# The first ffn's transposed input: turned again on TensorE, or read back from DRAM

## The chip, the cores and the metric

The kernel runs on one core of one Trainium2 chip. The core has five engines with a queue each: TensorE (PE, whose weight loads the profile lists as PEld), VectorE (DVE), ScalarE (ACT), GpSimd (POOL) and SyncE (SP, which here only issues DMAs). The metric is the device time of one execution in microseconds (us); less is better.

## What is computed

Two gated blocks follow each other, on x of 4 x 1024 rows with 512 elements. Each block is

```
xn = layernorm(x)
s  = attention(xn)          # layer 0: chunked linear attention, 16 heads; layer 1: softmax attention
g  = silu(ffn(xn))          # layer 0: below; layer 1: gated ffn with integer weights
x  = x + s * g
```

What the change touches is the input of layer 0's ffn:

```
def bitlinear(x, w):                       # used twice in the ffn: w_fc, then w_proj
    xn = (x - mean(x)) / sqrt(var(x) + 1e-6)
    return xn @ ternarize(w).T
h = gelu(bitlinear(xn, w_fc));  y = bitlinear(h, w_proj)
```

So the ffn normalises rows that layer 0's norm has already normalised. With the row's variance v, that is xn times one more factor per row, 1/sqrt(v/(v + 1e-5) + 1e-6).

## The kernel before, in words

The 4096 rows are worked on in NBLK = 8 blocks of BLK = 512 rows, a block in TPB = 4 tiles of 128 rows. The 512 elements of a row are KD = 4 pieces of 128, the contraction pieces of the matmuls.

**Layer 0's attention** (up to 622 us in the profile) goes through 32 steps, four head groups for each block. For each block, `moments0` (L292) takes mean and variance of the four tiles, `norms0` (L302) makes from them a factor that goes straight from x to the ffn's input (`st[:, :, 3]`), and `turn0` (L310) normalises a tile on DVE, turns it on TensorE and copies it with ACT into `xnT`, the transposed block that all projections of the attention read. Each step also makes on POOL the decayed queries `qd` (L357), which `outs` uses one step later, and for odd blocks a copy of the state (L395). The last step (L512 to L514) also prepares the first ffn block: `first_rows` (L453) scales each of four row tiles of x (loaded at L542) on DVE, turns it with four transposes (L463) and has `split_in` (L227) write it as a pair: `hi`, the value rounded to fp32r by ACT, and `lo`, the remainder, by DVE. Both are matmul operands. After it come the last `output` matmuls (L333).

**Layer 0's ffn** (622 to some 1150 us) is a software pipeline over g, 16 slots c = 0 to 15 for each block. In a slot, `hidden` (L587) does eight fc matmuls (L594, the pair hi and lo times four pieces), then on ACT gelu to h (L599), the rounding hp (L604) and the square (L606), on DVE the remainder hp (L607) and the sum of squares (L616), on POOL the sum of h (L615). `proj` (L642) does eight pj matmuls (L647) with the hp of two to eight slots before. PSUM gives fc two banks, h has three buffers. In slots 1, 3, 5, 7 `gate` (L652) finishes a row tile of the previous block: loads of x and s by SP (L659, L661), DVE L664, tanh on ACT L666, DVE L667 and L668, the add of x on POOL L669, the store of x1 by SP (L670), and DVE's bn_stats on it (L105). `stats` (L620) comes in slot 1. `turn_out` (L673), in slots 14 and 15 and the next block's 0 and 2, transposes the result for layer 1 (L684).

The next block's input is made in the same slots: in slots 0, 3, 6, 9 SP loads a row tile of x (`x0f`, L711); in slots 2, 5, 8, 11 `prep_in` (L566) scales it on DVE (`xq`, L574); in slots 3, 6, 9, 12 `turn_in` (L579) has TensorE transpose it (four 128 x 128 matmuls with the identity, L582) and `split_in` writes hi (ACT, L230) and lo (DVE, L231).

In block 0 the last six tiles of the projection's weights are made ternary on DVE beside it (L208, L210).

**What sets the order.** TensorE's order is the program's, written out by hand (`manual_schedule`). On the other engines a planner orders the instructions of each queue by its own estimate of when they are ready; an instruction wrapped in `keep_in_program_order` is put behind the one traced before it on its engine, but later ones may still be put ahead of it. Each engine then runs its queue strictly in order and waits at semaphores. SP's and POOL's DMAs stand in those queues too.

Of the kernel before, what the change touches and what calls it, by code (L numbers as in the profile page):

```python
# [24 lines left out]
NTILE = NT // P  # L25
BLK = 512
TPB = BLK // P
NBLK = NT // BLK
# [7 lines left out]
def kernel(ctx, tc, ins, out):  # L36
    nc = tc.nc
# [17 lines left out]
    def tr(name):  # L55
        return psum.tile([P, 4, P], F32, tag="tr", name=name)
# [6 lines left out]
    ident = const.tile([P, P], F32, tag="ident", name="ident")  # L63
# [15 lines left out]
    def xpair(name):  # L79
        return [xpool.tile([P, KD, BLK], F32, tag=f"xp{n}", name=f"{name}_{n}") for n in range(2)]  # L80
# [61 lines left out]
    def transpose_to(dst, src, name, on_scalar):  # L142

        t = tr(f"tr_{name}")
        for k in range(4):
            nc.tensor.transpose(t[:, k, :], src[:, k * P : (k + 1) * P], ident)
        if on_scalar:
            nc.scalar.copy(dst, t)  # L148
        else:
            nc.vector.tensor_copy(dst, t)  # L150
# [73 lines left out]
            w = nxt  # L224
            yield

    def split_in(xp, i, tp):  # L227

        hi, lo = [a[:, :, i * P : (i + 1) * P] for a in xp]
        nc.scalar.copy(hi.bitcast(F32R), tp)  # L230
        nc.vector.tensor_tensor(lo.bitcast(F32R), tp, hi, ALU.subtract)  # L231


    with ExitStack() as es:
# [6 lines left out]
        xt = {}  # L241
# [45 lines left out]


        xnTs, vs, oTs = {}, {}, {}
        xparts = {}  # L290

        def moments0(blk):  # L292
            st = st0[blk]
            for i in range(TPB):
# [7 lines left out]
        def norms0(blk):  # L302

            st = st0[blk]
            nc.vector.tensor_tensor(st[:, :, 3], st[:, :, 1], st[:, :, 1], ALU.mult)
            nc.vector.tensor_tensor(st[:, :, 3], st[:, :, 3], st[:, :, 2], ALU.mult)
            inv_std(st[:, :, 3], eps6)
            nc.vector.tensor_tensor(st[:, :, 3], st[:, :, 3], st[:, :, 1], ALU.mult)

        def turn0(blk, i):  # L310
            st = st0[blk]
            t = blk * TPB + i
            xn = p2.tile([P, D], F32, tag="xn", name=f"xn0_{t}")
            nc.vector.tensor_scalar(
                xn, xt.pop(t), st[:, i, 0:1], st[:, i, 1:2], ALU.subtract, ALU.mult
            )
            transpose_to(xnTs[blk][:, :, i * P : (i + 1) * P], xn, f"x0_{t}", True)

        def values(blk, i):
            if i == 0:  # L320
# [129 lines left out]
            oTs[blk, g] = p2.tile([P, BLK], F32, tag="oT", name=f"oT0_{nm}", bufs=6)  # L450
            nc.scalar.copy(oTs[blk, g], o)

        def first_rows(i0):  # L453

            st = st0[0]
            for i in range(i0, i0 + 2):
                xq = p2.tile([P, D], F32, tag="xn", name=f"xq_{i}")
                nc.vector.tensor_scalar(
                    xq, xt.pop(i), st[:, i, 0:1], st[:, i, 3:4], ALU.subtract, ALU.mult
                )  # L460
                tp = tr(f"tr_xq_{i}")
                for k in range(KD):
                    nc.tensor.transpose(tp[:, k, :], xq[:, k * P : (k + 1) * P], ident)  # L463
                split_in(xparts[0], i, tp)

        es.enter_context(tc.manual_schedule(engines={mybir.EngineType.PE}))

        st = st0[0]
# [37 lines left out]
        for n, (blk, g) in enumerate(steps):  # L506

            if g < 2:
                jobs = [(output, blk - 1, 2 * g + c) for c in range(2)] if blk else []
            else:  # L510
                jobs = [(values, blk + 1, 2 * g - 4 + c) for c in range(2)] if blk + 1 < NBLK else []
            if n + 1 == len(steps):  # L512
                xparts[0] = xpair("xp_0")
                jobs = [(first_rows, 0), (first_rows, 2)]  # L514
            if g == 0 and blk + 1 < NBLK:
                moments0(blk + 1)
            pts = scores(blk, g, *cur[:2])
            for _ in range(2):
                next(beside, None)
            nxt = None  # L520
            if n + 1 < len(steps):
                nxt = project(*steps[n + 1])
            if jobs:
                jobs[0][0](*jobs[0][1:])
            outs(blk, g, cur[2], pts)
            if nxt:
# [25 lines left out]
    with ExitStack() as es:  # L552
# [5 lines left out]
        def tr0(name):  # L558
            return pp.tile([P, KD, P], F32, tag="tr", name=name)

        hparts, sums, mvs, x1s, xnTp, x0fs = {}, {}, {}, {}, {}, {}
        for c in range(wpj0, NH0):
            wpj.append(p2.tile([P, D], F32R, tag=f"wpj{c}", name=f"wpj{c}", bufs=1))
        rows = p2.tile([P, D], F32, tag="rows", name="rows", bufs=1)

        def prep_in(blk, i):  # L566

            st = st0[blk]
            if i == 0:
                xparts[blk] = xpair(f"xp_{blk}")  # L570
            t = blk * TPB + i
            x = x0fs.pop(t)
            xq = p2.tile([P, D], F32, tag="xq", name=f"xq_{t}")
            nc.vector.tensor_scalar(  # L574
                xq, x, st[:, i, 0:1], st[:, i, 3:4], ALU.subtract, ALU.mult
            )
            return lambda: turn_in(blk, i, xq)

        def turn_in(blk, i, xq):  # L579
            tp = tr0(f"tr_xq_{blk}_{i}")  # L580
            for k in range(KD):
                nc.tensor.transpose(tp[:, k, :], xq[:, k * P : (k + 1) * P], ident)  # L582
            split_in(xparts[blk], i, tp)

        before = None

# [65 lines left out]
        def gate(blk, i):  # L652

            t = blk * TPB + i
            mv = mvs[blk]

            last = blk == NBLK - 1 and i >= 2
            x = p2.tile([P, D], F32, tag="x" if last else "xr", name=f"x0r_{t}")
            nc.sync.dma_start(out=x, in_=x_t[t])  # L659
            s = p2.tile([P, D], F32, tag="xq" if last else "s", name=f"s0_{t}")  # L660
# [7 lines left out]
            nc.vector.scalar_tensor_tensor(th, th, sc, s, ALU.mult, ALU.mult)  # L668
            nc.gpsimd.tensor_tensor(th, th, x, ALU.add)  # L669
            nc.sync.dma_start(out=x1_t[t], in_=th)  # L670
            moments(p2, th, st1[:, t, :], f"c{t}")
# [19 lines left out]
                )  # L691

        es.enter_context(tc.manual_schedule(engines={mybir.EngineType.PE}))
        pending = None
        W = {}
        for g in range(NH0 * NBLK + 2 + 2 * TPB):
            blk, c = divmod(g, NH0)
# [7 lines left out]
                        )  # L705
                    )
            if blk < NBLK:
                if c % 3 == 0 and c < 3 * TPB and blk + 1 < NBLK:
                    t = (blk + 1) * TPB + c // 3
                    x0fs[t] = p2.tile([P, D], F32, tag="x", name=f"x0f_{t}")  # L710
                    nc.sync.dma_start(out=x0fs[t], in_=x_t[t])  # L711
                if c >= 2 and c % 3 == 2 and c < 2 + 3 * TPB and blk + 1 < NBLK:
                    pending = prep_in(blk + 1, (c - 2) // 3)
                hidden(blk, c)
                if blk == 0 and wpj0 + c < NH0:
                    ternary("pj", wpj0 + c, raw0("pj", wpj0 + c, "f"))
            for i in range(TPB):
# [13 lines left out]
                gate(blk - 1, c // 2)  # L731
            if blk and c == 12:
                norm1(blk - 1, p2)
            if pending and c % 3 == 0:
                pending()
                pending = None
# [755 lines left out]
```

## Time and profile before

| | |
|---|---|
| time, median of 3 runs | 3141.68 us (3139.5 to 3142.14) |
| the profiled execution's own time | 3143.35 us |
| its span | 3141.6 us |
| TensorE clock granted, mean | 0.993 |
| layer 0's ffn, a whole block from slot 2 to slot 2 | 65.3 to 66.8 us |
| DVE's operations that the change takes out of the ffn | L574: 28, 731 ns in the mean; L231: 32 with the last step of the attention, 671 ns |
| TensorE's transposes of it | L582: 112, L463: 16 |
| HBM read / written | 104.10 MB / 41.94 MB |

The profile is of one execution. Its page gives each engine's busy time; the windows give the same for chosen stretches; the timeline gives single instructions: start and duration in us, engine, line, output and inputs, and in brackets how long the engine stood idle before it and what ended that. "x8" at the end of a row says that eight such instructions are merged in it. A TensorE row's duration contains the run of the pipeline; the time that a matmul takes from the engine is the distance between starts.

### The profile page before, as it was taken

The numbers are of one execution on the slowest core, as the hardware profiler recorded it, in microseconds if no ns is written. First come the engines' busy times: TensorE is split into PE (matmuls) and PEld (weight loads), VectorE is DVE, ScalarE is ACT, GpSimd is POOL, SyncE is SP. The second block draws the span as 40 slices with busy tenths as digits, with TensorE's granted clock in tenths as the row PEclk, the third lists the DMA queues.
The fourth block names the chain that finished last, engine by engine and source line by source line (L and its number), as shares of the span: only waits on it lengthen the run. The fifth ranks groups of instructions, "written<-read, shape, count | busy, mean of one in ns | idle before, by whom it ended". The sixth has DMA issues, their size and how long they took to land.

```text
span 3141.6 us, 60980 instructions
## 1 busy us (share of the span) xinstructions
PE 3083.5 (98%) x26185; PEld 1762.0 (56%) x26185; DVE 1898.5 (60%) x2622; ACT 1195.6 (38%) x1696; POOL 1501.6 (48%) x615
## 2 busy tenths in 40 slices
PE   9999999999999998999999999999999999999998
PEld 5555555577777874443344444334444435888887
DVE  4444555478887866566655555555555684566655
ACT  3111111155556543444444444444444444333332
POOL 0000000034444444888888898888888970000001
PEclk9999999999999999999999999999999999999999
DMA  3111111112222331100001000100000013322211
GB/s 131 54 54 61 54 54 41 58 54 87 84 74 68 108 127 49 35 9 8 8 17 40 13 11 15 41 14 14 10 17 15 12 44 104 115 77 64 68 51 55
DMA packets 97799, 158.46 MB, mean 50 GB/s; under 512 B 13040, under 2 KB 26864, under 8 KB 97392
## 3 DMA queue, kind: packets, MB, share of 16 engines
q1 hardware_dynamic: 96704, 151.33, 15.6%
q8 instruction: 207, 3.39, 0.5%
q0 software_dynamic: 816, 3.15, 0.3%
q14 instruction: 72, 0.59, 0.1%
HBM read 104.10 MB, written 41.94 MB: 46 GB/s over the span
## 4 chain that ended last, share of the span: by engine, by line
PE 84%; DVE 11%; ACT 2%; issue 2%; POOL 1%; SPq 1%; DMA 0%; ACTq 0%; POOLq 0%; DVEq 0%
PE sk L1033 9%; PE sq L1006 8%; PE y L1052 8%; PE qk L350 7%; PE gate L1224 5%; PE up L1224 5%; PE dn L1246 5%; PE v1ps L862 4%; PE v0ps L324 4%; PE wo L333 3%; PE wo L862 3%; PE wk L862 3%; PE wq L862 3%; PE fc L594 3%; PE pj L647 3%; PE sk L1039 2%
## 5 line engine op out<-in xcount | busy, mean ns | idle before, releaser
L1073 POOL TENSOR_TENSOR part<-part,pT 128x2048 f32<-128x2048 f32 x184 | 844.5, 4590 | 25.8 <-ACT pT L1044 16.8
L1010 DVE TENSOR_REDUCE mx<-sq 128x2 f32<-128x1024 f32 x512 | 603.3, 1217 | 384.1 <-PE sq L1006 383.0
L1044 ACT ACTIVATE pT<-sk 128x1024 f32<-128x1024 f32 x512 | 496.2, 1021 | 618.8 <-PE sk L1039 615.4
L1033 PE MATMUL sk<-wqT,wkT 32*128 32x512 f32 x2048 | 332.7, 645 | 5.2 <-DVE mx L1010 5.1
L1006 PE MATMUL sq<-wkT,wqT 32*128 32x512 f32 x2048 | 322.9, 642 | 7.1 <-ACT pT L1044 5.1
L1052 PE MATMUL y<-pT,v 128*32 128x512 f32 x2048 | 276.3, 610 | 0.2 <-ACT pT L1044 0.2
L615 POOL TENSOR_TENSOR sums<-sums,h 128x512 f32<-128x512 f32 x112 | 164.2, 1466 | 227.3 <-ACT h L599 222.1
L647 PE MATMUL pj<-wpj,hp 128*128 128x512 f32 x1024 | 265.1, 397 | 5.7 <-DVE hp L607 4.9
L594 PE MATMUL fc<-xp,wfc 128*128 128x512 f32 x1024 | 260.9, 397 | 2.9 <-ACT h L599 2.0
L1268 POOL TENSOR_TENSOR th<-th,x 128x512 f32<-128x512 f32 x31 | 40.1, 1293 | 457.9 <-DVE th L1267 377.1
L1039 PE MATMUL sk<-mT,onesr 2*128 2x512 f32 x1024 | 239.8, 788 | 2.2 <-DVE mT L1022 2.2
L357 POOL TENSOR_TENSOR qd<-qT,wqkv 128x512 f32<-128x512 f32 x32 | 40.6, 1270 | 397.5 <-ACT qT L355 372.3
L350 PE MATMUL qk<-xnT,wqkv 128*128 128x512 f32 x512 | 229.9, 602 | 0.7 <-ACT xnT L148 0.7
L647 PEld LDWEIGHTS pj<-wpj,hp 128*128 128x128 f32 x1024 | 190.2, 188 | 57.6 <-DVE hp L607 17.3
L594 PEld LDWEIGHTS fc<-xp,wfc 128*128 128x128 f32 x1024 | 187.5, 188 | 44.2 <-ACT h L599 5.1
L1033 PEld LDWEIGHTS sk<-wqT,wkT 32*128 32x128 f32 x2048 | 99.7, 184 | 138.3 <-issue 110.4
L1071 POOL TENSOR_TENSOR part<-pT,pT 128x2048 f32<-128x2048 f32 x31 | 141.1, 4552 | 74.4 <-ACT pT L1044 74.3
L1224 PE MATMUL gate<-xp,wf 128*128 128x512 f32 x704 | 174.2, 390 | 0.0
L1224 PE MATMUL up<-xp,wf 128*128 128x512 f32 x704 | 173.9, 389 | 0.0
L1246 PE MATMUL dn<-wf,hp 128*128 128x512 f32 x704 | 173.6, 389 | 0.0
L607 DVE TENSOR_TENSOR hp<-h,hp 128x512 fp32r<-128x512 f32 x128 | 118.0, 922 | 76.3 <-ACT hp L604 76.2
L350 PEld LDWEIGHTS qk<-xnT,wqkv 128*128 128x128 f32 x512 | 95.5, 191 | 112.4 <-issue 106.3
(219 smaller groups left out, 4527.0 us busy)
## 6 DMA issues: line engine op xcount, KB each, us to landing
s<-s SPq DMA_DIRECT2D x96, 256.0 KB
x<-x SPq DMA_DIRECT2D x36, 256.0 KB
x<-in_x SPq DMA_DIRECT2D x32, 256.0 KB
raw_fc<-in_w_fcT SPq DMA_DIRECT2D x32, 256.0 KB
x0f<-in_x SPq DMA_DIRECT2D x32, 256.0 KB
x0r<-in_x SPq DMA_DIRECT2D x32, 256.0 KB
x<-th SPq DMA_DIRECT2D x32, 256.0 KB
xnT<-xnT_d SPq DMA_DIRECT2D x8, 1024.0 KB
```

What stands on the lines that cost most here:

```text
L350: nc.tensor.matmul(a, lhsT=wqkv[k][:, c0 : c0 + P], rhs=xnTs[blk][:, k, :], start=(k == 0), stop=(k == KD - 1),)
L594: nc.tensor.matmul(a, lhsT=wfc[k][:, c * P : (c + 1) * P], rhs=xp[n][:, k, :].bitcast(F32R), start=(k == 0 and n == 0), stop=(k == KD - 1 ...
L647: nc.tensor.matmul(ds[i], lhsT=hparts[blk, c][n][:, i * P : (i + 1) * P], rhs=wpj[c], start=(c == 0 and n == 0), stop=(c == NH0 - 1 and n ...
L862: nc.tensor.matmul(out[r0 : r0 + HD, :], lhsT=lhsT[:, r0 : r0 + HD], rhs=rhs, start=start, stop=stop,)
L1006: nc.tensor.matmul(sq[:, hh, :], lhsT=qT[r, q0 : q0 + P], rhs=kT[r, n * 512 : (n + 1) * 512], start=True, stop=True,)
L1010: nc.vector.tensor_reduce(mx[:, qt, 2 * pair : 2 * pair + 2, n], sq, AX.X, ALU.max)
L1033: nc.tensor.matmul(sks[h // 2][:, h % 2, :], lhsT=kT[r, kb * P : (kb + 1) * P], rhs=qT[r, qh * 512 : (qh + 1) * 512], start=True, stop=False,)
L1044: nc.scalar.activation(pT[:, 2 * pair : 2 * pair + 2, :], sks[pair], AF.Exp, scale=QKS)
L1052: nc.tensor.matmul(y[r, :], lhsT=v[:, kb, r], rhs=pT[:, h, :], start=(kb == 0), stop=(kb == TB - 1),)
L1073: add.tensor_tensor(parts[u], parts[u], pT, ALU.add)
L1224: nc.tensor.matmul(a, lhsT=ws[n, c][:, k, :], rhs=xp[m][:, k, :], start=(k == 0 and m == 0), stop=(k == KD - 1 and m == 1),)
L1246: nc.tensor.matmul(ds[i], lhsT=hparts[blk, c][n][:, i * P : (i + 1) * P], rhs=w, start=(c == 0 and n == 0), stop=(c == NH1 - 1 and n == 1),)
```

## The change

The transposed rows that the attention makes anyway are kept. When the last tile of a block is turned, POOL's DMA queue stores the whole `xnT` of the block (1 MB) to a new DRAM tensor `xn0T`; another of its DMAs stores the factor of each row (512 values, now without the first norm's factor in it) to `more`. The ffn's input is then made from these, piece by piece (k = 0 to 3, all 512 rows of 128 elements at once) instead of row tile by row tile: SP loads piece k in slot 3k (and, with the first, the factors, broadcast to 128 partitions); POOL multiplies it by the factors in slot 3k + 3, three slots after its load; in slot 3k + 4 ACT writes hi and POOL writes lo. Loads, scales and splits are kept in program order. For the first block the loads come after the attention's last step but one, and the scales and splits at the end of the last step. TensorE's transposes L463 and L582, DVE's scaling L458 and L574, and DVE's split L231 are no longer there.

```
+    xn0T_d = [
+        dram.tile([KD, P, BLK], F32, tag=f"xn0T{i}", name=f"xn0T_d{i}") for i in range(NBLK)
+    ]
+    more_d = dram.tile([NBLK, BLK], F32, tag="more", name="more_d")
...
-    def split_in(xp, i, tp):
...
+    def ffn_in(blk, k, tile):
+
+        if k == 0:
+            xparts[blk] = xpair(f"xp_{blk}")
+            mores[blk] = tile("more", f"more_{blk}")
+            nc.sync.dma_start(out=mores[blk], in_=more_d[blk].partition_broadcast(P))
+        x = tile("x", f"x0f_{blk}_{k}")
+        tc.keep_in_program_order(nc.sync.dma_start(out=x, in_=xn0T_d[blk][k]))
+
+        def scale():
+            tc.keep_in_program_order(nc.gpsimd.tensor_tensor(x, x, mores[blk], ALU.mult))
+
+        def split():
+            hi, lo = [a[:, k, :] for a in xparts[blk]]
+            tc.keep_in_program_order(nc.scalar.copy(hi.bitcast(F32R), x))
+            tc.keep_in_program_order(
+                nc.gpsimd.tensor_tensor(lo.bitcast(F32R), x, hi, ALU.subtract)
+            )
+
+        return scale, split
...
@@ norms0
-            nc.vector.tensor_tensor(st[:, :, 3], st[:, :, 3], st[:, :, 1], ALU.mult)
+            nc.gpsimd.dma_start(out=more_d[blk].rearrange("(i p) -> p i", p=P), in_=st[:, :, 3])
@@ turn0
             transpose_to(xnTs[blk][:, :, i * P : (i + 1) * P], xn, f"x0_{t}", True)
+            if i == TPB - 1:
+                nc.gpsimd.dma_start(out=xn0T_d[blk].rearrange("k p n -> p k n"), in_=xnTs[blk])
...
-        def first_rows(i0):
...
             if n + 2 == len(steps):
 
-                for i in range(TPB):
-                    xt[i] = p2.tile([P, D], F32, tag="x", name=f"x0f_{i}", bufs=4)
-                    tc.keep_in_program_order(nc.sync.dma_start(out=xt[i], in_=x_t[i]))
+                first_in = [
...
+                    for k in range(KD)
+                ]
+            if n + 1 == len(steps):
+                for m in range(2):
+                    for k in range(KD):
+                        first_in[k][m]()
...
-        def prep_in(blk, i):
...
-        def turn_in(blk, i, xq):
...
             if blk < NBLK:
-                if c % 3 == 0 and c < 3 * TPB and blk + 1 < NBLK:
...
-                    nc.sync.dma_start(out=x0fs[t], in_=x_t[t])
-                if c >= 2 and c % 3 == 2 and c < 2 + 3 * TPB and blk + 1 < NBLK:
-                    pending = prep_in(blk + 1, (c - 2) // 3)
                 hidden(blk, c)
+                if blk + 1 < NBLK and c <= 3 * KD + 1:
+                    if c % 3 == 0 and c:
+                        coming[0]()
+                    if c % 3 == 0 and c < 3 * KD:
+                        nxt = ffn_in(
+                            blk + 1, c // 3,
+                            lambda tag, name: p2.tile([P, BLK], F32, tag=tag, name=name),
+                        )
+                    if c % 3 == 1:
+                        if c > 1:
+                            coming[1]()
+                        coming = nxt
...
-            if pending and c % 3 == 0:
-                pending()
-                pending = None
```

More of the change, by code (lines that the diff above doesn't have):

```diff
@@ L225, in weights0 @@
             yield
-    def split_in(xp, i, tp):
-        hi, lo = [a[:, :, i * P : (i + 1) * P] for a in xp]
-        nc.scalar.copy(hi.bitcast(F32R), tp)
-        nc.vector.tensor_tensor(lo.bitcast(F32R), tp, hi, ALU.subtract)
+    def ffn_in(blk, k, tile):
[14 more added lines that the diff above has]
+        return scale, split
+    xparts, mores = {}, {}
     with ExitStack() as es:
@@ L289 @@
         xnTs, vs, oTs = {}, {}, {}
-        xparts = {}
         def moments0(blk):
@@ L451, in outs @@
             nc.scalar.copy(oTs[blk, g], o)
-        def first_rows(i0):
[L455 to L464, printed above, removed]
         es.enter_context(tc.manual_schedule(engines={mybir.EngineType.PE}))
@@ L511 @@
                 jobs = [(values, blk + 1, 2 * g - 4 + c) for c in range(2)] if blk + 1 < NBLK else []
-            if n + 1 == len(steps):
-                xparts[0] = xpair("xp_0")
-                jobs = [(first_rows, 0), (first_rows, 2)]
             if g == 0 and blk + 1 < NBLK:
@@ L538 @@
             if n + 2 == len(steps):
-                for i in range(TPB):
-                    xt[i] = p2.tile([P, D], F32, tag="x", name=f"x0f_{i}", bufs=4)
-                    tc.keep_in_program_order(nc.sync.dma_start(out=xt[i], in_=x_t[i]))
+                first_in = [
+                    ffn_in(
+                        0, k,
+                        lambda tag, name: p2.tile(
+                            [P, BLK], F32, tag={"more": "xn"}.get(tag, tag), name=name,
+                            bufs={"x": 4}.get(tag, 2),
+                        ),
+                    )
[5 more added lines that the diff above has]
+                        first_in[k][m]()
         for i in range(TPB):
@@ L559, in tr0 @@
             return pp.tile([P, KD, P], F32, tag="tr", name=name)
-        hparts, sums, mvs, x1s, xnTp, x0fs = {}, {}, {}, {}, {}, {}
+        hparts, sums, mvs, x1s, xnTp = {}, {}, {}, {}, {}
         for c in range(wpj0, NH0):
@@ L564 @@
         rows = p2.tile([P, D], F32, tag="rows", name="rows", bufs=1)
-        def prep_in(blk, i):
[L568 to L577, printed above, removed]
-        def turn_in(blk, i, xq):
[L580 to L583, printed above, removed]
         before = None
@@ L659, in gate @@
             nc.sync.dma_start(out=x, in_=x_t[t])
-            s = p2.tile([P, D], F32, tag="xq" if last else "s", name=f"s0_{t}")
+            s = p2.tile([P, D], F32, tag="more" if last else "s", name=f"s0_{t}")
             nc.sync.dma_start(out=s, in_=s0_t[t])
@@ L707 @@
             if blk < NBLK:
-                if c % 3 == 0 and c < 3 * TPB and blk + 1 < NBLK:
-                    t = (blk + 1) * TPB + c // 3
-                    x0fs[t] = p2.tile([P, D], F32, tag="x", name=f"x0f_{t}")
-                    nc.sync.dma_start(out=x0fs[t], in_=x_t[t])
-                if c >= 2 and c % 3 == 2 and c < 2 + 3 * TPB and blk + 1 < NBLK:
-                    pending = prep_in(blk + 1, (c - 2) // 3)
-                hidden(blk, c)
+                hidden(blk, c)
+                if blk + 1 < NBLK and c <= 3 * KD + 1:
[5 more added lines that the diff above has]
+                            lambda tag, name: p2.tile([P, BLK], F32, tag=tag, name=name),
+                        )
+                    if c % 3 == 1:
+                        if c > 1:
+                            coming[1]()
+                        coming = nxt
                 if blk == 0 and wpj0 + c < NH0:
@@ L733 @@
                 norm1(blk - 1, p2)
-            if pending and c % 3 == 0:
-                pending()
-                pending = None
             if 0 < blk < NBLK and c >= 14:
```

## The prediction

> **What bounds the kernel.** I read the granted clock first (0.993, so nothing is throttled), then the page's busy times, then, by windows, the stage that the change touches: the first ffn, 622 to 1150 us.
>
> ```profile
> PE 3083.5 (98%) x26185; PEld 1762.0 (56%) x26185; DVE 1898.5 (60%) x2622; ACT 1195.6 (38%) x1696; POOL 1501.6 (48%) x615
> ```
>
> TensorE is busy all the time, so whatever leaves it should shorten the kernel, unless another engine is the one that paces a stretch. I number a block's slots c = 0 to 15 (one group of eight fc and eight pj matmuls each). From the first fc of slot 2 to that of slot 13 (the gate of the previous block lies there) the windows of blocks 1 to 7 are:
>
> ```profile
> core 0: us, PE busy (x) PEld busy (x) DVE busy (x) ACT busy (x) POOL busy (x), PEclk, DMA share, GB/s
> 690.87:734.68 43.81, 43.14 (x195) 34.46 (x194) 40.06 (x64) 23.79 (x40) 23.41 (x15) 1.00 0.31 91
> 756.21:801.24 45.03, 44.03 (x198) 34.70 (x198) 41.15 (x64) 24.34 (x41) 23.12 (x15) 1.00 0.35 111
> 822.78:867.81 45.03, 44.07 (x199) 34.70 (x198) 41.15 (x64) 24.32 (x41) 23.06 (x15) 1.00 0.35 112
> 889.35:934.64 45.29, 44.33 (x198) 34.62 (x198) 41.13 (x64) 24.32 (x41) 23.05 (x15) 1.00 0.37 111
> 956.19:1001.21 45.02, 44.10 (x199) 34.69 (x198) 41.14 (x64) 24.32 (x41) 23.06 (x15) 1.00 0.36 111
> 1022.75:1067.36 44.61, 43.78 (x198) 34.78 (x198) 40.49 (x64) 24.36 (x41) 22.73 (x15) 1.00 0.36 113
> 1088.90:1131.44 42.54, 41.82 (x182) 33.35 (x182) 36.48 (x59) 22.68 (x38) 22.16 (x15) 1.00 0.31 100
> ```
>
> DVE is busy 41 of 45 us: it has no room. The last row prepares no next block, so it is a trial of the removal made inside this profile. An undisturbed slot takes 3.67 us (fc starts 834.80 and 838.47) and one with four transposes 4.13 (879.75 to 883.88), so 0.45 us for a set. TensorE alone would need 11 x 3.67 + 0.45 = 40.8 us in the last row; it took 42.54. Even without input work it waits 1.7 us, and for this:
>
> ```profile
> 1119.91 1.80 DVE L668 SCALAR_TENSOR_TENSOR th<-th,mv,s 128x512 f32<-128x512 f32 x1
> 1121.64 0.68 DVE L607 TENSOR_TENSOR hp<-h,hp 128x512 fp32r<-128x512 f32 x1
> 1122.24 1.77 DVE L616 TENSOR_TENSOR sums<-sums,sq 128x512 f32<-128x512 f32 x1
> ```
> ```profile
> 1119.87 1.30 POOL L615 TENSOR_TENSOR sums<-sums,h 128x512 f32<-128x512 f32 x1 [3.28 <-ACT h L599]
> 1121.79 1.67 POOL L669 TENSOR_TENSOR th<-th,x0r 128x512 f32<-128x512 f32 x1 [0.63 <-DVE th L668]
> ```
> ```profile
> 1122.37 1.89 PE L647 MATMUL pj<-wpj,hp 128*128 128x512 f32 x7 [0.25 <-DVE hp L607]
> ```
>
> These are the timelines of DVE, POOL and PE. A DVE operation with two SBUF inputs that meets a POOL operation takes 1.8 us, the same one free of it 0.68 (L616, L607) or 0.74 (L668); the hp that this holds back is what pj waits for. In these slots the stage is paced by DVE, and POOL lengthens DVE.
>
> **The change part by part.**
>
> Removed on PE: 28 sets of L582 transposes, 0.45 us each, 12.6 us, and 4 sets of L463. The latter's second pair stands bare at the end of the attention (wait from 605.7, next matmul 607.28): 1.6 us. The first pair lies beside DVE's pt (602.09 to 604.57), for which PE waits anyway: nothing.
>
> Removed on DVE: per block four xq (L574, 731 ns mean) and four splits (L231, 671 ns), 5.6 us, three of each in the gate window. What that is worth the last row says: 42.54 against 45.0 us (mean of blocks 2 to 6) is 2.5 us, of which four transposes are 1.8; the DVE operations, partly lying in its waits for ACT's th (3.1 us), give only 0.7. L308 (8 x 565 ns) goes too, in the attention, where DVE waits for PE: 0. ACT's cast stays, from SBUF instead of PSUM (L803 619 ns against L230 575): 4 x 0.05 us per block beside 38 busy of 66: 0.
>
> Added on POOL: per block four scales and four subtractions, 128x512 two-input fp32, as L615 (1.29 us alone). No row shows POOL writing fp32r; on DVE the type costs nothing (L607 as L616), so I take 1.29. POOL has room, busy 28 of a block's 66 us. The price is what they do to DVE. In the last row's window the excess of DVE's operations over their free times is 10 x (1.118-0.68) + 11 x (0.977-0.68) + 4 x (1.538-0.74) = 10.9 us for 15 POOL operations: 0.72 us each. The Trainium skill (SBUF — State Buffer, Who interferes with whom) has it harder: the pair of ports is locked for a whole instruction and the loser blocks fully. By that rule an added operation may cost up to 1.29 us, and six in slots 3 to 10 7.7 us a block; by the row 6 x 0.72 = 4.3. The lower end is 0, where the operation meets DVE reading PSUM (y L664, 734 ns always) or waiting. I take the row: same operations, same slots. Scale and subtraction of slots 12 and 13 meet a DVE that has caught up: 0.
>
> Added waits: the subtraction waits on POOL for ACT's cast, which stands behind h, hp and sq of its slot; queued behind it are the next sums and the gate's add (L669), for which DVE's bn_stats (L105) waits, with hp behind it and pj behind that. In the sum this counts as 0 beyond the 0.72; the third case prices it. The cast waits for a scale that is a slot older: 0.
>
> SP: a block gets five loads (four and the broadcast) for four, at 0.33 us issue. Pinned behind the gate's stores (issued 834.36, 849.92, 859.12 in block 3's gate), a load lands some 2.4 us later (as x0r does in the chain), 7 to 10 us before the sums of the slot whose scale takes it: hidden; cover gone, the scale, the sums behind it and the free h buffers would be late. SP's stores of x1 are not moved.
>
> The stores, on POOL's queue in the attention: 8 of 1 MB and 8 of 2 KB in 4-byte pieces. The three weight loads there issue in 0.75 to 0.91 us and land in 5.7 to 9.4. For the small ones no row is near; between 0 and a few us I take 0.9. They are read some 500 us later. Behind them on POOL stand qd (L357) and the state copy (L395), which idle 372 and 154 us for their inputs in all, and qd is used a step (18 us) later. Taken at 0; the upper end, every issue late for PE, is 16 x 0.9 = 14 us, which qd's idle time excludes nearly wholly.
>
> The sum, in us. Blocks 1 to 6: before 268.8 (the six rows); after, by the last row, 42.1 (block 1 has one transpose set less) + 5 x 42.54 + 6 x 4.3 = 280.6: +11.8. Block 0 has no gate: 4 x 0.45 of transposes and PE's one 1.88 wait for xq go, two POOL operations meet DVE's ternary work (2 x 0.72): -2.3. End of the attention -1.6. In all +7.9. The profiled execution took 3143.35 (span 3141.6 and 1.75 around it) and would take 3151.3; it is 1.7 above the median, so on the median 3149.6, say 3150.
>
> **The rivals.**
>
> *Faster: POOL's operations fall in gaps.* Place: slots 3 to 10. POOL idles 21 us of the last window, much of it while DVE does y, bn_stats or waits for ACT. At 1 us a block instead of 4.3: 254.8 + 6 - 268.8 = -8.0, block 0 -3.7, attention -1.6: 3128; at 0, 3122. It decides below 3.0 us a block, 0.5 per operation, where the sum is zero. For it: six of the last window's ten L616 are free. Against: h, which starts sums, also starts hp, and the pinned operations follow sums directly, when DVE's two-input work runs.
>
> *Slower still: the gate's add behind a waiting subtraction.* If in slots 4 and 7 the queue has the subtraction first, L669 comes 1.3 us later twice a block: 6.9 us a block, 254.8 + 41.4 - 268.8 - 3.9 = +23.5: 3165. For it: bn_stats already waits for L669 once (1.2 us, last row). Against: the subtraction may be queued behind L669.
>
> *It does nothing that shows:* DVE's order is changed and the price comes out near 3.0: 3142.
>
> **How the numbers follow.** Sum as reckoned 0.45 (3143 to 3158), gaps 0.30 (3122 to 3136), late add 0.17, nothing 0.08. About 0.2% is what a measurement of this kernel tells from no change, 3135 to 3148: gaps give faster 0.29; same takes the last case and the lower edge of the first, 0.19; slower 0.52. Range over the signs 3124 to 3166; the likeliest case's own is 3143 to 3158.
>
> **What would show it.** Right: L582, L574, L231 gone; windows from slot 2 to 13 of blocks 1 to 6 near 46.8 us with PE waiting for hp L607; L616, L607 and L668 longer in the mean; last block unchanged at 42.5; fc starting 1.6 us earlier than 622.05. Gaps: windows at 43 to 44. Late add: waits of L105 for L669 over 1 us per block. Wrong altogether: PE waiting for xp or SP's loads, or for qd in the attention, or POOL's fp32r operation well over 1.3 us.

## The result, and the profile after

| | before | after |
|---|---|---|
| median (runs shown beside each other) | 3141.2 us (4 runs, 3139.5 to 3142.1) | 3182.8 us (4 runs, 3171.7 to 3186.4) |
| ratio, 95% interval | | 1.0129 (1.0115 to 1.0143) |
| profiled execution: time, span | 3143.35, 3141.6 us | 3171.73, 3170.0 us |
| first fc | 622.05 us | 624.14 us |
| block 0, from first fc to slot 2 of block 1 | 68.82 us | 69.21 us |
| blocks 1 to 6, from slot 2 to slot 2 | 398.0 us | 429.4 us |
| from slot 2 of block 7 to the end | 2052.7 us | 2047.2 us |

The change made the kernel 1.3% slower, outside the forecast range. The four rows below are differences of starts in the two traces: +2.1, +0.4, +31.4 and -5.5 us, together the 28.4 us between the spans. The last one lies where no operation was changed, only the name of one buffer. The changed kernel, measured once more (last experiment), took 3176.5 us; by the two ratios the loss is some 34 to 41 us.

The page of after, engines' busy time and number of instructions:

```profile
PE 3068.1 (97%) x26057; PEld 1745.7 (55%) x26057; DVE 1927.3 (61%) x2550; ACT 1196.9 (38%) x1696; POOL 1624.1 (51%) x695
```

TensorE lost its 128 transposes and 15 us of busy time. DVE lost 72 operations and is busy 29 us longer: the operations that stayed grew. That alone says where to look.

The windows of after: blocks 1 to 3 and 7 from slot 2 to slot 13, as in the prediction, and slot 14 of block 2 alone.

```profile
core 0: us, PE busy (x) PEld busy (x) DVE busy (x) ACT busy (x) POOL busy (x), PEclk, DMA share, GB/s
697.57:743.00 45.43, 41.49 (x176) 32.38 (x175) 41.56 (x46) 23.85 (x40) 33.85 (x22) 1.00 0.29 93
764.03:810.94 46.91, 42.39 (x182) 33.16 (x182) 41.15 (x57) 24.36 (x41) 31.17 (x20) 1.00 0.34 108
835.79:882.73 46.94, 42.38 (x183) 33.15 (x182) 41.16 (x57) 24.36 (x41) 31.22 (x20) 1.00 0.33 108
1122.75:1165.29 42.54, 41.82 (x182) 33.32 (x182) 36.48 (x59) 22.66 (x38) 22.17 (x15) 1.00 0.31 100
814.61:822.05 7.44, 4.25 (x22) 3.23 (x20) 6.96 (x18) 2.19 (x4) 3.73 (x3) 1.00 0.11 35
```

The gate's window takes 46.9 us, as forecast (46.8), against 45.0 before: DVE is as busy as before (41.15 us) with fewer operations (57 for 64). The last block is the same to the hundredth. But the window is less than half of the loss: a block is 5.2 us longer (71.76 against 66.57) and the window only 1.9. The other 3.3 us are slot 14, 7.44 us against 4.03 in block 2 of before (slot 13 gives 0.1 us back). There TensorE's fc starts are 805.01 and 809.04, and the transposes between them wait for nothing:

```profile
805.01 1.99 PE L594 MATMUL fc<-xp,wfc 128*128 128x512 f32 x8
806.83 2.02 PE L647 MATMUL pj<-wpj,hp 128*128 128x512 f32 x8
808.69 0.60 PE L684 MATMUL tr_x<-ident,xn 128*128 128x128 f32 x4
809.04 2.09 PE L594 MATMUL fc<-xp,wfc 128*128 128x512 f32 x8
```

The chain of slot 14 in after, from the timelines of TensorE, ACT, DVE and POOL in block 2:

```profile
816.43 2.02 PE L645 MATMUL pj<-wpj,hp 128*128 128x512 f32 x8
821.64 0.66 PE L682 MATMUL tr_x<-ident,xn 128*128 128x128 f32 x4 [3.19 <-ACT xn L677]
```
```profile
820.77 1.52 ACT L677 ACTIVATE xn<-th,shift,st 128x512 f32<-128x512 f32 x2 [5.18 <-DVE shift L143]
```
```profile
810.29 1.78 DVE L605 TENSOR_TENSOR hp<-h,hp 128x512 fp32r<-128x512 f32 x1
812.00 1.78 DVE L614 TENSOR_TENSOR sums<-sums,sq 128x512 f32<-128x512 f32 x1
813.70 1.79 DVE L605 TENSOR_TENSOR hp<-h,hp 128x512 fp32r<-128x512 f32 x1
815.41 1.78 DVE L614 TENSOR_TENSOR sums<-sums,sq 128x512 f32<-128x512 f32 x1
817.12 1.25 DVE L125 TENSOR_SCALAR rw_n<-st 128x4 f32<-128x4 f32 x1
...
820.57 0.16 DVE L143 SCALAR_TENSOR_TENSOR shift<-st 128x4 f32<-128x4 f32 x1
```
```profile
809.79 3.45 POOL L613 TENSOR_TENSOR sums<-sums,h 128x512 f32<-128x512 f32 x2
813.19 1.75 POOL L242 TENSOR_TENSOR x0f<-x0f,more 128x512 f32<-128x512 f32 x1
814.91 1.74 POOL L613 TENSOR_TENSOR sums<-sums,h 128x512 f32<-128x512 f32 x1
816.60 1.73 POOL L248 TENSOR_TENSOR xp<-x0f,xp 128x512 fp32r<-128x512 f32 x1
```

Read upwards from TensorE: the transposes of the finished tile wait 3.19 us for ACT's xn, this for DVE's `shift`, the last operation of norm1 (L125 to L143, here from 817.12), and norm1 stands behind hp and sums of slots 11 and 12, each at 1.78 us instead of 0.68. Even its first operation, of 128 x 4 elements, takes 1.25 us instead of 0.16: it ends when POOL's does. POOL beside them runs without a gap, each operation at 1.74 instead of 1.29. The starts on both engines are 1.7 us apart: the two take turns. So a POOL operation here costs DVE 1.7 - 0.6 = 1.1 us, and POOL is late as well: the last scale and subtraction, planned for slots 12 and 13, run in slots 13 and 14 (which begin at 810.94 and 814.61).

### The profile page after: what moved, and what is told of

The parts are those of the page before. It is cut to its first block, busy times and chain, and to the rows that moved or that the text cites. A ratio compares the mean times of both kernels' runs of the same rounds, so it can differ in the third digit from the quotient of the medians.

```text
span 3170.0 us, 60776 instructions
## 1 busy us (share of the span) xinstructions
PE 3068.1 (97%) x26057; PEld 1745.7 (55%) x26057; DVE 1927.3 (61%) x2550; ACT 1196.9 (38%) x1696; POOL 1624.1 (51%) x695
## 4 chain that ended last, share of the span: by engine, by line
PE 80%; DVE 10%; issue 4%; ACT 2%; POOL 2%; DMA 1%; SPq 1%; ACTq 0%; POOLq 0%; DVEq 0%
PE sk L1033 9%; PE sq L1006 8%; PE y L1052 8%; PE qk L372 7%; PE gate L1224 5%; PE up L1224 5%; PE dn L1246 5%; PE v1ps L862 4%; PE wo L355 3%; PE wo L862 3%; PE wq L862 3%; PE wk L862 3%; PE v0ps L346 3%; DVE sums L614 3%; PE fc L592 3%
## 5 line engine op out<-in xcount | busy, mean ns | idle before, releaser
L592 PE MATMUL fc<-xp,wfc 128*128 128x512 f32 x1024 | 259.6, 396 | 14.7 <-ACT h L597 13.9
L605 DVE TENSOR_TENSOR hp<-h,hp 128x512 fp32r<-128x512 f32 x128 | 154.4, 1206 | 71.6 <-ACT hp L602 71.6
```

What stands on the lines that cost most here:

```text
L592: nc.tensor.matmul(a, lhsT=wfc[k][:, c * P : (c + 1) * P], rhs=xp[n][:, k, :].bitcast(F32R), start=(k == 0 and n == 0), stop=(k == KD - 1 ...
```

## The experiments

The theory after the result: POOL's added operations lengthen DVE's two-input ones (port theory), first in the gate, then, through norm1, in slot 14. The rival: the pinned operations and their waits hold up POOL's queue (queue theory), and norm1 is only put in an unlucky place. The later start is put down to the stores (start theory). Ratios are to the kernel before, measured beside each; block lengths are the median of blocks 2 to 6 in the traces, from slot 2 to slot 2.

| kernel | time, us | ratio, 95% interval | a block, us | first fc, us |
|---|---|---|---|---|
| before | 3141.2 | | 66.6 | 622.05 |
| after | 3182.8 | 1.0129 (1.0115 to 1.0143) | 71.7 | 624.14 |
| before + stores | 3147.9 | 1.0012 (1.0004 to 1.0019) | 66.6 | 625.96 |
| after, no scale and subtraction | 3127.3 | 0.9951 (0.9935 to 0.9968) | 64.0 | 627.86 |
| after, memsets in their places | 3127.6 | 0.9949 (0.9932 to 0.9965) | 64.0 | 626.65 |
| after, both on DVE | 3141.5 | 0.9997 (0.9987 to 1.0007) | 66.75 | 628.19 |
| after, norm1 in slot 10 | 3166.1 | 1.0077 (1.0055 to 1.0100) | 70.05 | 625.19 |
| after, subtraction on DVE | 3163.6 | 1.0065 (1.0043 to 1.0088) | 69.1 | 626.41 |
| after, late stores, not held | 3178.7 | 1.0120 (1.0098 to 1.0141) | 71.7 | 624.10 |
| after, late stores, held | 3170.3 | 1.0103 (1.0085 to 1.0121) | 71.7 | 621.27 |
| split in the attention | 3122.0 | 0.9938 (0.9921 to 0.9955) | 64.0 | 622.64 |
| the same, factors held | 3125.0 | 0.9950 (0.9937 to 0.9963) | 64.0 | 623.38 |
| after, once more | 3176.5 | 1.0109 (1.0089 to 1.0128) | 71.7 to 73.2 | 627.07 |

The first fc is read from one trace each, and it carries something besides the change: TensorE's granted clock between 12 and 20 us was 0.62 to 1.00 in these 13 traces, and with it the first projection took 10.1 to 7.1 us.

**Before with the stores alone.** Nothing reads what they write.

```
+            nc.gpsimd.dma_start(out=more_d[blk].rearrange("(i p) -> p i", p=P), in_=st[:, :, 3])
...
+            if i == TPB - 1:
+                nc.gpsimd.dma_start(out=xn0T_d[blk].rearrange("k p n -> p k n"), in_=xnTs[blk])
```

> The kernel before, with only the new stores added in the attention (8 of 1 MB and 8 of 512 four-byte pieces, from POOL's queue); nothing reads them, the ffn is as before. Start theory (the first block's stores delay the weights' and constants' landing in the first 40 us): the second projection starts near 41.7 us instead of 38.0, time +3.6 us, 3145; nothing more later in the attention. Rival (the stores hold up qd or state copies in every block): +1 us or more for each of 8 blocks, 3150 or above. If the stores are free: 3141.

Measured: first fc 3.9 us later, blocks 1 to 6 as before (397.9 against 398.0 us); block 0 is 1.5 us longer in this trace, which wasn't followed up. Of the 3.9 us, u's wait for kd is 2.6 us (3.51 against 0.95), and 1.3 us lies ahead of that, most of it the first projection at a lower granted clock (0.64 against 0.80 between 12 and 20 us). Over all runs the ratio puts the stores' cost between 1.3 and 6 us. The loss of blocks 1 to 6 has nothing to do with them.

**Without the scale and the subtraction.** The factor is left out, and lo is a second cast of x by ACT instead of the remainder; loads, waits and ACT's cast stay.

```
-            tc.keep_in_program_order(nc.gpsimd.tensor_tensor(x, x, mores[blk], ALU.mult))
+            pass
...
-            tc.keep_in_program_order(
-                nc.gpsimd.tensor_tensor(lo.bitcast(F32R), x, hi, ALU.subtract)
-            )
+            tc.keep_in_program_order(nc.scalar.copy(lo.bitcast(F32R), x))
```

> The changed kernel with POOL's scale left out and lo written by a second cast on ACT instead of POOL's subtraction (it leaves out the factor and the remainder); loads, stores and hi stay. If POOL's 64 operations are the cause, as port conflict or as queue: slot 2 to 13 near 42.5 us in blocks 1 to 6 as in the last block, slot 14 back at 4.1 us, about 3124. If the loads, the casts on ACT or the stores are the cause: still near 3175.

Measured: a block falls from 71.7 to 64.0 us, slot 14 is back at 4.04. These eight operations are the whole of the ffn's loss and of the gain that was there: 7.8 us a block.

**POOL writes instead of reading.** Two memsets of about 0.53 us each in the place of each operation (x and lo become constants), so POOL's queue has the same waits in the same places and is held for 1.06 us by each pair, where the operation alone takes 1.29.

```
-            tc.keep_in_program_order(nc.gpsimd.tensor_tensor(x, x, mores[blk], ALU.mult))
+            for _ in range(2):
+                tc.keep_in_program_order(nc.gpsimd.memset(x, 0.5))
...
-            tc.keep_in_program_order(
-                nc.gpsimd.tensor_tensor(lo.bitcast(F32R), x, hi, ALU.subtract)
-            )
+            for _ in range(2):
+                tc.keep_in_program_order(nc.gpsimd.memset(lo, 0.0))
```

> The changed kernel with each scale and each subtraction replaced by two POOL memsets of the same tile (it leaves out the factor and the remainder): POOL is as long in the way of its queue, with the same waits for ACT's cast, but reads no SBUF. Port theory (DVE's two-input operations are blocked by POOL's reads): L605 and L614 fall back towards 0.68 to 1.1 us, slot 14 without its 3.3 us wait, 3124 to 3132. Queue theory (the gate's add and the sums come late behind the new operations): L605 and L614 may fall, but slots 7 to 9 and 14 keep their waits, 3165 to 3180.

The groups of hp and of the sum of squares between 690 and 1125 us, of before, of after, then of this kernel (number, busy us, mean ns, idle before):

```profile
L607 DVE TENSOR_TENSOR hp<-h,hp 128x512 fp32r<-128x512 f32 x105 | 92.2, 878 | 58.4 <-ACT hp L604 58.4
L616 DVE TENSOR_TENSOR sums<-sums,sq 128x512 f32<-128x512 f32 x91 | 103.6, 1138 | 0.0
```
```profile
L605 DVE TENSOR_TENSOR hp<-h,hp 128x512 fp32r<-128x512 f32 x97 | 120.5, 1242 | 55.6 <-ACT hp L602 55.6
L614 DVE TENSOR_TENSOR sums<-sums,sq 128x512 f32<-128x512 f32 x84 | 115.3, 1372 | 0.0
```
```profile
L605 DVE TENSOR_TENSOR hp<-h,hp 128x512 fp32r<-128x512 f32 x109 | 115.7, 1062 | 64.5 <-ACT hp L602 64.5
L614 DVE TENSOR_TENSOR sums<-sums,sq 128x512 f32<-128x512 f32 x96 | 89.4, 931 | 0.0
```

And one stretch of this kernel's POOL and DVE, block 2:

```profile
792.02 1.30 POOL L613 TENSOR_TENSOR sums<-sums,h 128x512 f32<-128x512 f32 x1
793.26 1.11 POOL L249 MEMSET xp<- 128x512 f32 x2
```
```profile
792.08 1.79 DVE L605 TENSOR_TENSOR hp<-h,hp 128x512 fp32r<-128x512 f32 x1
793.79 0.68 DVE L614 TENSOR_TENSOR sums<-sums,sq 128x512 f32<-128x512 f32 x1
```

hp, which starts with a POOL operation that reads, takes 1.79 us; sums, which lies inside the memsets, 0.68. The queue theory falls: waits and nearly as much occupied time are still there (the 24 casts of ACT in this stretch wait 17.1 us for POOL, 14.7 in after), and the loss is gone: 3127.6 us, a block at 64.0. The Trainium skill (SBUF — State Buffer, Who interferes with whom) has it so: a DVE instruction with two SBUF inputs "contends with a GpSimd instruction that reads SBUF, not with one that only writes it".

**Both on DVE.**

```
-            tc.keep_in_program_order(nc.gpsimd.tensor_tensor(x, x, mores[blk], ALU.mult))
+            tc.keep_in_program_order(nc.vector.tensor_tensor(x, x, mores[blk], ALU.mult))
...
-                nc.gpsimd.tensor_tensor(lo.bitcast(F32R), x, hi, ALU.subtract)
+                nc.vector.tensor_tensor(lo.bitcast(F32R), x, hi, ALU.subtract)
```

> The changed kernel with scale and subtraction on DVE instead of POOL. Port theory: eight operations of 0.68 us a block take the place of what DVE did before (5.6 us a block), POOL does what it did before, so slot 2 to 13 near 43 to 45 us and slot 14 near 4.1: 3130 to 3143, against 3172 to 3183 for the change. If DVE's own load is what hurts, not POOL's: 3160 or above.

Measured: 41 us faster than after, level with before. DVE carries eight more operations a block (scale 1.20 us in the mean, subtraction 0.68) and the block is still 5 us shorter: POOL takes more from DVE than doing the same work costs DVE itself.

**norm1 in slot 10.**

```
-            if blk and c == 12:
+            if blk and c == 10:
```

> The changed kernel with norm1 issued in slot 10 instead of slot 12; nothing else. If the wait in slot 14 (3.2 us of PE for xn, six times) is only a matter of where norm1's sixteen small operations stand in VectorE's queue, slot 14 falls from 7.4 to about 4.1 us and the run to 3183 - 20 = about 3163. If VectorE is simply behind in slots 12 to 14 whatever stands first, the wait moves to pj for hp of slots 11 to 13, less than a third comes back, and the run stays above 3175.

Each theory was half right. TensorE's timeline:

```profile
813.90 1.88 PE L645 MATMUL pj<-wpj,hp 128*128 128x512 f32 x7 [1.42 <-DVE hp L605]
819.32 0.60 PE L682 MATMUL tr_x<-ident,xn 128*128 128x128 f32 x4
```

The wait for xn is gone and slot 14 is at 4.06 us, but in slot 13 pj now waits 1.42 us for hp, which norm1 has moved back (5.36 us instead of 3.67). A block gains 1.7 of the 3.3 us, which over six blocks is 10 of the 16.7 us between the medians; the rest is about the 6 us by which the two medians of after differ (last experiment).

**The subtraction alone on DVE.**

```
-                nc.gpsimd.tensor_tensor(lo.bitcast(F32R), x, hi, ALU.subtract)
+                nc.vector.tensor_tensor(lo.bitcast(F32R), x, hi, ALU.subtract)
```

> The changed kernel with the subtraction on VectorE and the scale still on GpSimd: four instead of eight GpSimd operations a block that read SBUF beside VectorE. Port theory: about half of the loss of 55 us against the kernel without these operations comes back, less VectorE's own 4 x 0.7 us a block: 3155 to 3165, between 3141 (both on VectorE) and 3183. A theory in which only a threshold counts (VectorE's backlog at slot 12) gives either end: below 3145 with slot 14 at 4 us, or above 3178 with slot 14 still over 7.

3163.6, within the port theory's span. A block takes 69.1 us: half of POOL's operations gone, half of the way to the 66.75 with none. No threshold shows.

**Block 0's stores later, first try.** The two stores were written at the second step of the attention.

```
+            if n == 1:
+                store_more(0)
+                nc.gpsimd.dma_start(out=xn0T_d[0].rearrange("k p n -> p k n"), in_=xnTs[0])
```

> The changed kernel, but block 0's two stores are issued at the second step of the attention instead of in the lead-in. If they are what delays the second projection by 3.7 us, u no longer waits 3.2 us for kd there, the first fc starts at about 620.5 instead of 624.1, and the run takes 3183 - 3.7 = about 3179. If the delay came from elsewhere, the first fc stays at 624 and the time at 3183.

First fc at 624.10 as if nothing was done, and nothing was: POOL still issued them at 11.7 and 12.6 us. The planner moves up what waits for nothing, wherever it is written. The run tells nothing of the cause.

**Block 0's stores held back.** DVE copies the factors, and one column of xnT onto itself, in the second step, and the stores read the copies.

```
+            if n == 1:
+                late = p2.tile([P, TPB], F32, tag="late", name="late", bufs=1)
+                tc.keep_in_program_order(nc.vector.tensor_copy(late, st0[0][:, :, 3]))
+                one = xnTs[0][:, 0, 0:1]
+                tc.keep_in_program_order(nc.vector.tensor_copy(one, one))
...
```

> The same as the run before it with late stores, but now held back in fact: in that run both stores of block 0 still went out at 11.7 and 12.6 us, since nothing they read came later. Here VectorE copies the factors (and one column of the rows onto itself) in the second step, and the stores read the copies. If the stores delay the lead-in, u's wait of 3.2 us is gone, first fc at 620.5 instead of 624.1, and the run at about 3179; if they don't, first fc stays at 624.

What the start waits for, in u's row of TensorE's timeline, after and then this kernel:

```profile
39.49 1.16 PE L410 MATMUL u<-v,kd 128*128 128x128 f32 x8 [3.19 <-DVE kd L396]
41.68 7.13 PE L372 MATMUL qk<-xnT,wqkv 128*128 128x512 f32 x16
```
```profile
34.46 1.16 PE L416 MATMUL u<-v,kd 128*128 128x128 f32 x8 [0.94 <-DVE kd L402]
36.65 7.13 PE L378 MATMUL qk<-xnT,wqkv 128*128 128x512 f32 x16
```

DVE does kd behind the product `dec`, that waits for ACT, and ACT in after for a constant of 192 KB still under way:

```profile
29.77 4.78 ACT L500 ACTIVATE dec<-cst,slb 128x128 f32<-128x128 f32 x16 [5.13 <-DMA cst<-in_c_decay]
```

In before the same activation ran at 21.34, in this kernel at 22.46. The DMA rates in slices of 1.5 us from 0 to 60 us show why: before, after, and the kernel of the next experiment, which at the start stores the factors but not the rows:

```profile
GB/s 0 191 354 361 365 378 392 403 391 304 142 223 388 404 397 342 53 11 0 0 0 0 0 0 5 0 0 0 0 0 146 247 265 223 175 4 0 268 82 0
```
```profile
GB/s 0 212 292 347 348 391 396 396 377 327 96 27 40 79 102 232 377 405 393 385 373 196 8 0 0 0 5 0 0 0 0 0 8 317 242 142 60 44 40 27
```
```profile
GB/s 0 202 292 330 361 378 404 395 384 288 158 128 44 52 56 111 358 404 401 391 133 5 0 0 0 5 0 0 0 0 0 157 264 266 75 14 55 31 29 163
```

From 15 to 22.5 us, while the factors' 4-byte pieces are written, the rate in after falls to 27 to 102 GB/s, where before has 142 to 404; what is left of the constants and the 1 MB of rows follow. With the factors alone the rate falls as well, to 44 to 128 GB/s from 16.5 to 24 us, where before has 223 to 404. In the nine kernels with both stores at the start `dec` begins between 29.8 and 32.7 us and the second projection between 41.66 and 45.10. The start theory holds: held back, u waits 0.94 us, in before 0.95.

That wait is 2.25 of the 5.0 us by which the second projection is earlier here. The other 2.8 us are no effect of the stores that a run shows. They lie in the first projection, which took 9.88 us in after and 7.13 here (8.73 in before), and in the granted clock (the figure before the DMA share) between 12 and 20 us. These are the rows of before, after, this kernel and after once more:

```profile
12.00:20.00 8.00, 8.00 (x15) 3.59 (x16) 0.34 (x2) 2.37 (x4) 0.00 (x0) 0.80 0.97 296
12.00:20.00 8.00, 7.76 (x12) 3.44 (x13) 0.17 (x1) 1.44 (x3) 1.45 (x2) 0.64 1.22 170
12.00:20.00 8.00, 7.79 (x18) 3.53 (x19) 0.34 (x2) 3.15 (x6) 0.00 (x0) 1.00 0.92 256
12.00:20.00 8.00, 7.91 (x19) 3.61 (x20) 0.17 (x1) 2.00 (x3) 1.51 (x2) 1.00 1.27 179
```

The last has both stores at the start and the full clock: the clock does not follow the stores. Its second projection began at 44.62 all the same, with `dec` at 32.71. The time of this kernel, 3170.3, is 9 us below the 3179 expected; no more than 3 us of the gain stand at the first fc (621.27), and the rest isn't traced.

**Scale and split in the attention.** There DVE is busy half of the time and POOL a tenth. Two pieces in each of a block's last two steps (in the last block one step earlier); both parts are stored by SP, and the ffn loads them straight into the operand pair.

```
+        def split0(blk, k):
+            if k == 0:
+                nc.sync.dma_start(out=more, in_=more_d[blk].partition_broadcast(P))
...
+            tc.keep_in_program_order(
+                nc.gpsimd.tensor_tensor(x, xnTs[blk][:, k, :], more, ALU.mult)
+            )
...
+            nc.scalar.copy(hi.bitcast(F32R), x)
+            tc.keep_in_program_order(
+                nc.gpsimd.tensor_tensor(x.bitcast(F32R), x, hi, ALU.subtract)
+            )
+            nc.sync.dma_start(out=xpT_d[blk][0, k], in_=hi)
+            nc.sync.dma_start(out=xpT_d[blk][1, k], in_=x)
...
     def ffn_in(blk, k):
...
+                nc.sync.dma_start(
+                    out=xparts[blk][n][:, k, :], in_=xpT_d[blk][n, k]
+                )
```

> Scale and split of every block are done in the attention, where VectorE is busy half of the time and GpSimd a tenth: two pieces in each of a block's last two steps (GpSimd scales, ScalarE rounds, GpSimd subtracts), both parts are stored in DRAM, and the first ffn only loads them; block 0's factors are stored after the lead-in. Port theory: the ffn's blocks take 64.0 us as in the kernel without the GpSimd operations (71.7 with), the attention stays at PE's 99% with u's first wait gone, so that the first fc starts at about 620.5: 3127 less 3 to 7, so 3120 to 3126, faster than both kernels. If loads into the ffn or stores (twice the bytes) are what costs, or GpSimd in the attention holds VectorE up there too, it comes out at 3140 or more.

3122.0 us, 0.6% faster than before and 1.9% than after (3122.0 / 3182.8 = 0.981). The windows of the attention, after and then this kernel:

```profile
300.00:450.00 150.00, 148.76 (x942) 82.79 (x941) 79.38 (x162) 21.23 (x36) 14.57 (x16) 1.00 0.24 68
```
```profile
300.00:450.00 150.00, 148.76 (x942) 82.73 (x941) 81.99 (x162) 25.77 (x44) 31.72 (x30) 1.00 0.30 87
```

POOL is busy 17 us more and DVE 2.6 us more with as many operations, so some collide here too, but TensorE's 148.76 us don't change: it is the bound, and DVE has room. In the ffn a block takes 64.0 us. The factors' store was written later but went out at 11.81 us like the others. Alone it delays `dec` to 26.83 us, but u waits no longer than in before (0.94 us against 0.95): the second projection, at 39.47, is late because the first took 10.11 us at a granted clock of 0.62.

**The same with the factors held back,** as above, for all blocks.

```
+            if g == 1:
+                late = p2.tile([P, TPB], F32, tag="late", name=f"late_{blk}", bufs=1)
+                tc.keep_in_program_order(nc.vector.tensor_copy(late, st0[blk][:, :, 3]))
...
+            if g == 2:
+                for k in range(2 if blk + 1 < NBLK else 4):
```

> The kernel that scales and splits in the attention, with block 0's factors held back in the same way (all blocks store them from a copy made in the block's second step). In the version without this the 2 KB of factors alone delayed the lead-in: rates fell to 44 to 130 GB/s for 8 us where before had 390, and the second projection began at 39.5 instead of 38.0. Expected: second projection at 38.0, first fc 1.4 us earlier (621.2), time 3120 to 3121, which its noise of 3 us would hide; if the factors' store is not the cause, the second projection stays at 39.5.

`dec` moved to 21.33 us and the second projection to 36.58, more than expected. But u waits 0.94 us in both kernels; the 2.9 us between them are the first projection, 7.13 us at a granted clock of 1.00 here. So the expectation was wrong about the cause: the factors' store alone had delayed no projection. What was gained was given back: the last block's four pieces now stand in one step, and there `outs` waits 2.71 us for ACT's kT (0.57 in the kernel without this) and the granted clock is 0.50 from 597.4 to 600.8 us, so that the first fc came at 623.38. 3125.0 against 3122.0 is no difference that these runs tell.

**After once more.**

> The changed kernel once more, unaltered. Its profiled execution took 3171.7 us, its other three 3182.7 to 3186.4. If the traced causes are the whole of the loss, they give 34 us on before (2.1 at the first fc, 0.4 in block 0, 31.4 in blocks 1 to 6), a median of about 3175, with the rest of the program spread by some 5 us either way by the granted clock. If something more of the change lies in layer 1, where no line was touched, the median stays at 3180 to 3186 with the stretch after the ffn longer than before's 2010 us in the trace.

3176.5 us, close to what the traced causes give, and 2045.5 us from slot 2 of the last block to the end against 2052.7 in before. Layer 1 takes no part in the loss. That its first four runs lay 6 us higher in the median isn't traced: three of them have no trace, and their granted clock was 0.990 to 0.991 against the profiled one's 0.995.

## Why the prediction was wrong

The mechanism was the right one, its extent was not. By its own steps, on the profiled executions (+7.9 forecast, +33.9 traced up to slot 2 of the last block):

- *What the removal is worth:* right. Without POOL's operations a block is 2.6 us shorter than before (64.0 against 66.6), forecast 2.5; the end of the attention gave its 1.6 us (the first fc is 2.1 us later where the second projection is 3.65 later).
- *Six operations in slots 3 to 10 at 0.72 us:* right, 46.9 us against 46.8. The window without them is 42.5, so 4.4 us for six, 0.73 each. They ran later than planned, in slots 4 to 12.
- *"Scale and subtraction of slots 12 and 13 meet a DVE that has caught up: 0."* This step failed. Slots 13 to 1, outside the window, are 3.3 us longer a block, 20 us in all, most of the miss. After the gate DVE had not caught up: scale and subtraction came about a slot late on a POOL that was itself stretched, met the sums and hp back to back, and norm1 came behind them. With norm1 earlier the wait went to hp and half of it stayed, so it was a backlog and not only a place in the queue. The forecast had taken the price per operation from a window in which 15 POOL operations leave gaps. Over all eight it was 7.8 / 8 = 0.98 us, and 1.1 where POOL ran without a gap, nearer to 1.29 us, the estimate that I had worked out from the Trainium skill's page (SBUF — State Buffer, Who interferes with whom) and set aside.
- *The stores, taken at 0:* wrong, by 2.25 us of u's wait in this pair of traces. I bounded them by what stands behind them in POOL's queue, and that part held; I did not ask what else was on its way at 12 us, when the constants of the first step were still landing. The other 1.4 us of the 3.65 at the second projection lie ahead of that wait, most of them in the first projection, which took 9.88 us instead of 8.73 at a lower granted clock (0.64 instead of 0.80 between 12 and 20 us); no run ties that to the change. The 0.993 that I read as "nothing is throttled" is a mean over 3141 us; it doesn't show the first microseconds.
- *Block 0, -2.3:* it came out at +0.4. I counted two of POOL's operations as meeting DVE; without all of them block 0 takes 65.2 us, 4 less, half a microsecond for each of the eight.
- *The rivals:* gaps did not come. The sign given for the late add did: in every block of after L110 waits once for L667, 1.18 to 1.19 us, where before has this only in block 7. But the kernel without the scale and the subtraction has the same wait in every block at 64.0 us a block, so it is not what was lost, and the sign was a poor one. The forecast of 3165 lay nearest for another reason. That the range ended at 3166 came from treating the after-gate slots as free of cost in every case.

11.8 + 19.6 of blocks 1 to 6, -2.3 + 2.7 of block 0, -1.6 + 3.7 of the start (1.4 of it ahead of u's wait) make +33.9.

## What to carry to other kernels

When work is moved to a free GpSimd, count it twice: its own time, and what its SBUF reads add to every two-input VectorE operation beside it; where GpSimd then runs without a gap, take the whole turn (1.1 us for a 128x512 operation here), and follow the delay beyond the stretch in which VectorE is full, to the next short chain behind it. The same operations were free where TensorE alone was the bound and VectorE half idle, so here another stage (3122.0 us) was worth more than another engine (3141.5). A store in the lead-in competes with the loads that the lead-in waits for, and an early store written late in the program is not late until something it reads is. And before a shift in the first microseconds is put down to a change, compare the granted clock there: the mean over the run hides it.

## What the runs showed of the hardware beyond that

- A GpSimd memset (0.53 us) beside a two-input VectorE operation cost it nothing (0.68 us), where a reading operation made it 1.79.
- GpSimd writing fp32r is no slower than fp32: 1.70 us for the subtraction in the mean against 1.74 for the scale, both in contention.
- Beside 2 KB stored in 4-byte pieces all DMA together ran at 44 to 128 GB/s from 16.5 to 24 us, where before had 223 to 404; with the rows' store behind it, at 27 to 102 from 15 to 22.5 us. With that store alone in the lead-in ACT's `dec` came 5.5 us later than with it held back (26.83 and 21.33). The Trainium skill (DMA: Bandwidth & Descriptors, Rules for kernel authors) says that a non-contiguous last dimension takes a descriptor for each element; the trace counts packets, 64 for this store, so no run here shows the descriptors.
